# Two graph layers, 16 batches: the partition sums of the first and last batches leave TensorE

## The chip, the cores and the metric

The kernel runs on one core of a Trainium2 chip. Its time is the device time of one launch in microseconds (us). Five engines run their own instruction streams in order: TensorE (PE in the profile), VectorE (DVE), ScalarE (ACT), GpSimd (POOL), and SyncE (SP), which issues the transfers. An engine waits for another only where an instruction needs its result or a buffer that it has still to give back.

## The reference

The input is `x` of 16 batches, 1024 nodes and 256 channels in float32, and one 1024x1024 matrix `adj`. Two layers follow each other in each batch:

```python
# layer 0, per batch
fea  = x.T;  c = mean(fea, axis=channels)
A    = 2*abs(abs(sigmoid(c[None,:]-c[:,None]) - .5) - .5)
Wg   = adj * (A + A.T)/2
q    = relu((fea @ Wg) * para)                # 4 heads of 64
k, v = split(x @ kv_w)
x    = layernorm(x + softmax(q k^T * scale) v)
# layer 1, per batch
h    = relu(x @ w1_loop + adj @ (x @ w1_neigh) + b1)
h    = relu(h @ w2_loop + adj @ (h @ w2_neigh) + b2)
x    = layernorm(x + (x + h)/2)
```

The change concerns the divisors of the softmax (one sum of exponentials for each node and head) and the mean and variance of the first layer's norm (one of each for each node).

## The kernel before

All tensors are cut into tiles of 128 partitions. In layer 0 the norm works in a blocked layout: 128 partitions are four blocks ("quarters") of 32, and a node's channels are spread over the four partitions that have the same place in each block, and over columns. The columns are summed by VectorE. That leaves a `[128, 32]` or `[128, 64]` tile of parts, and one sum over the four quarters is still open, whose result all four need. The divisors of the softmax are spread in the same way, with the two heads of a pair in the two halves of 64 partitions.

There are two ways of closing that sum before the change.

- *By TensorE*, with a constant 128x128 matrix `fold` (L185 to L188) which has a one where two partitions have the same place in their block. `fold_sums` (L283) multiplies a part by it; `denominators` (L862) and `add` (L910) do the same for the divisors and take the reciprocals from PSUM in two halves of 64 partitions (L873, L922). Each such product shows in the profile as two records. The lines are L286, L867 and L916.
- *Without TensorE.* `den_shift` (ScalarE copies each half of 64 partitions to the other half's place in a PSUM tile), `den_halves` (VectorE adds the two), `den_quarters` (four ScalarE copies exchange neighbouring blocks of 32, then VectorE adds and takes the reciprocal), L875 to L897; and `across` (L289), the same pattern for means and variances on GpSimd alone.

One loop over the batches (in `run`, L1456 to L1757) writes out the order of every engine by hand; nothing reorders it. In batch `b`'s turn the kernel works on the attention of batch `b`, the queries, keys and values of batch `b + 1`, and the graph convolutions of batches `b − 1` and `b − 2`, so that TensorE finds work of one while the other engines are at another. The turns are of four kinds, by what neighbours exist:

- batch 0 (`more and not c1`), L1546 and L1654: no convolutions yet; its queries go column by column (`q.step`, products at L633);
- batch 1 (`more and not both`), L1556 and L1712: one convolution;
- batches 2 to 14, L1590 and L1692: the steady turn, which already closes its sums without TensorE;
- batch 15 (`else`), L1650 and L1730: no next batch, so no queries, keys or values.

After the loop come the last convolutions and norms (L1741 to L1757).

Batches 0, 1 and 15 use `fold`: 4, 6 and 4 products. Their places matter. In batch 0 they stand between the query products; the variance's (`norm.variance`, L385) comes just before `kv.sums`, VectorE's four sums for the next keys (L450 to L458), and GpSimd then raises the variance to the power −1/2 (L388) for `norm.scale` (L393). In batch 15 the denominators of the first pair of heads follow the attention outputs (`att.add_pairs(0)`), those of the second pair the first adjacency product of `Joined.run` (L1385), and the mean and variance stand after its products 6 and 7 (the keys 6 and 5 of the dictionary handed to it).

PSUM has two kinds of tiles here: three "big" ones of 1024 columns and two "bank" ones of 512. `scores` (L755) uses both: with `first` given, one score tile in four is split over the two banks (L761 to L763). Scratch for the sums is taken from the banks too.

`Joined.run` computes the two joined convolutions from seven products (numbered 1 to 7) in three PSUM tiles; ScalarE copies each finished product out (L1403 to L1422) so that the tile can be used again, and one of these copies, L1403, puts the loop term of batch `b − 1` into the third tile before product 2 adds to it.

## Time and profile before

| what | value |
|---|---|
| median of 3 runs | 2105.44 us (2105.36 to 2105.63) |
| the profiled execution | 2104.63 us |
| its span | 2102.8 us |
| mean granted TensorE clock | 0.999 of full speed |
| turns of batches 0 and 1 and the start (0 to 320 us) | TensorE busy 317.5, VectorE 286.9, ScalarE 187.2, GpSimd 35.3 us |
| a steady stretch (440 to 560 us) | TensorE 119.9, VectorE 108.1, ScalarE 73.0, GpSimd 28.2 us |
| last turn (1940 to 2062 us) | TensorE 120.4, VectorE 102.3, ScalarE 47.7, GpSimd 17.0 us |

A line of a timeline reads: start in us, busy us, engine, line of the kernel, operation, output <- inputs, partitions x columns, type, count; in brackets the idle time ahead of it and what ended it. Consecutive instructions of one form are drawn together, so "x8" is eight of them. Busy times of neighbours on one engine overlap a little, since an instruction is counted until its last write. The chain of waits is followed back from the last instruction: it gives each engine the share of the span for which it was what the end waited for.

### The profile page before, as it was taken

To read this page: it belongs to the slowest core of one execution; us is meant where nothing else is said; L and a number is where in the kernel's file an instruction comes from. 1 tells how busy PE (TensorE), PEld (TensorE's weight loads), DVE (VectorE), ACT (ScalarE), POOL (GpSimd) and SP (SyncE) were. 2 spreads that over 40 slices of the span, in tenths; PEclk is the share of its full clock that TensorE was granted. 3 is DMA by queue.
4 is the path that set the end of the run, shared out by engine and by line. 5 is a ranking of instruction groups with operands and counts; after the bars stand their busy time and mean duration, and the time that the engine had idled before them with its cause. 6 is when DMAs were issued, how large, how long until landed. Compare 5 with 4: busy or idle time off the path is not lost.

```text
span 2102.8 us, 24938 instructions
## 1 busy us (share of the span) xinstructions
PE 2090.7 (99%) x8282; PEld 988.5 (47%) x8282; DVE 1875.1 (89%) x2238; ACT 1265.9 (60%) x2190; POOL 425.5 (20%) x444
## 2 busy tenths in 40 slices
PE   9999999999999999999999999999999999999998
PEld 5354434445354453544535444354443534445355
DVE  7899998989989899898998989899899998989875
ACT  5844575556756576565755757557575585655523
POOL 2011103122031221213122031220312203122022
PEclk9999999999999999999999999999999999999999
DMA  9495756766648776477864768656586674966455
GB/s 216 122 178 189 145 140 205 138 216 146 173 168 161 242 135 192 151 146 244 142 216 139 135 232 162 230 120 146 206 176 217 143 147 183 185 212 136 137 184 187
DMA packets 688695, 364.99 MB, mean 174 GB/s; under 512 B 550704, under 2 KB 629936, under 8 KB 688560
## 3 DMA queue, kind: packets, MB, share of 16 engines
q1 hardware_dynamic: 688288, 363.07, 66.8%
q8 instruction: 67, 1.10, 0.2%
q14 instruction: 68, 0.56, 0.1%
q10 hardware_dynamic: 272, 0.26, 0.0%
HBM read 305.46 MB, written 57.80 MB: 173 GB/s over the span
## 4 chain that ended last, share of the span: by engine, by line
PE 94%; DVE 4%; issue 1%; DMA 0%; ACT 0%; SPq 0%; DVEq 0%; POOLq 0%; POOL 0%
PE av L815 20%; PE s L769 20%; PE hu_ps L1382 17%; PE g_ps L714 16%; PE v_ps L475 5%; PE k_ps L471 5%; PE hu_ps L1174 4%; PE g_ps L633 3%; PE in_ps L1037 1%; DVE xT L253 1%; DVE den_part L803 1%; DVE acc L790 1%; PE h_ps L1085 1%; PE u_ps L1114 1%; PE h_ps L1174 1%
## 5 line engine op out<-in xcount | busy, mean ns | idle before, releaser
L790 DVE TENSOR_TENSOR acc<-acc,pr 128x1024 f32<-128x1024 f32 x384 | 481.3, 1253 | 34.0 <-ACT pr L776 0.5
L769 PE MATMUL s<-qT,kT 64*128 64x512 f32 x2048 | 452.2, 594 | 1.6 <-DVE in L1054 0.7
L815 PE MATMUL av<-pr,v 128*64 128x512 f32 x2048 | 447.0, 594 | 0.0
L776 ACT ACTIVATE pr<-s 128x1024 f32<-128x1024 f32 x392 | 392.7, 1119 | 60.0 <-PE s L769 60.0
L769 PEld LDWEIGHTS s<-qT,kT 64*128 64x128 f32 x2048 | 194.2, 187 | 247.1 <-issue 186.6
L815 PEld LDWEIGHTS av<-pr,v 128*64 128x64 f32 x2048 | 144.1, 137 | 297.3 <-issue 265.7
L1382 PE MATMUL hu_ps<-adj,R 128*128 128x512 f32 x480 | 213.6, 592 | 0.0
L625 DVE SCALAR_TENSOR_TENSOR wg<-wg,adj 128x1024 f32<-128x1024 f32 x128 | 167.9, 1350 | 3.6 <-ACT wg L620 3.6
L774 ACT ACTIVATE pr<-s 128x512 f32<-128x512 f32 x240 | 142.6, 705 | 0.0
L619 ACT ACTIVATE wg<-c_row,c_sums 128x1024 f32<-128x1024 f32 x120 | 139.4, 1162 | 3.0 <-DVE accB L797 1.0
L1382 PEld LDWEIGHTS hu_ps<-adj,R 128*128 128x128 f32 x480 | 90.0, 190 | 107.1 <-issue 105.7
L620 ACT ACTIVATE wg<-wg 128x1024 f32<-128x1024 f32 x128 | 135.4, 1057 | 4.1
L388 POOL TENSOR_TENSOR rstd<-rstd,neg_half 128x32 f32<-128x32 f32 x16 | 88.3, 5520 | 147.4 <-DVE rstd L385 146.3
L1235 POOL TENSOR_TENSOR rstd<-rstd,neg_half 128x8 f32<-128x8 f32 x12 | 19.7, 1640 | 440.4 <-DVE rstd L1234 440.4
L714 PE MATMUL g_ps<-wg,x 128*128 128x512 f32 x224 | 107.7, 593 | 0.0
L1373 POOL TENSOR_TENSOR R<-h 128x512 f32<-128x512 f32 x14 | 19.6, 1397 | 435.3 <-PE av L815 408.7
L1382 PE MATMUL hu_ps<-adj,t 128*128 128x512 f32 x240 | 107.1, 598 | 0.0
L714 PE MATMUL g_ps<-T,xB 128*128 128x512 f32 x208 | 106.2, 592 | 0.0
L714 PE MATMUL g_ps<-wg,xB 128*128 128x512 f32 x208 | 106.2, 592 | 0.0
L788 DVE TENSOR_TENSOR acc<-pr,pr 128x1024 f32<-128x1024 f32 x64 | 78.0, 1218 | 14.8 <-ACT pr L776 14.8
L797 DVE STREAM_TRANSPOSE accB<-acc 128x1024 f32<-128x1024 f32 x64 | 79.7, 1245 | 3.5 <-PE av L815 0.5
L880 ACT COPY den<-den_part 64x64 f32<-64x64 f32 x26 | 5.5, 210 | 122.7 <-DVE den_part L803 122.2
(316 smaller groups left out, 3339.3 us busy)
## 6 DMA issues: line engine op xcount, KB each, us to landing
adj<-adjT SPq DMA_DIRECT2D x210, 512.0 KB
adj<-in_adj_dram SPq DMA_DIRECT2D x128, 512.0 KB
para<-in_L_gnn_para_dram SPq DMA_DIRECT2D x32, 512.0 KB
xB_a<-in_x_dram SPq DMA_DIRECT2D x128, 128.0 KB
x1d<-xB_a SPq DMA_DIRECT2D x128, 128.0 KB
x<-x1d SPq DMA_DIRECT2D x16, 1024.0 KB
xB<-in_x_dram SPq DMA_DIRECT2D x120, 128.0 KB
x<-in_x_dram SPq DMA_DIRECT2D x15, 1024.0 KB
```

The costliest lines, as they stand in the source:

```text
L471: nc.tensor.matmul(dst, self.a[0][n], self.w[n], start=not again, stop=True, skip_group_check=again)
L475: nc.tensor.matmul(dst[:, ts(t, P)], self.w[n][:, ts(t, P)], self.a[1][n], start=not again and t == 0, stop=True, skip_group_check=again o ...
L619: nc.scalar.activation(wg, self.c_row, AF.Abs, bias=self.c_col[:, t:t + 1], scale=-1.0)
L620: nc.scalar.activation(wg, wg, AF.Tanh, scale=-0.5 / C)
L625: nc.vector.scalar_tensor_tensor(wg, wg, 1.0, self.adj.pop(t), op0=ALU.add, op1=ALU.mult)
L714: nc.tensor.matmul(self.p[n], x_n[:, k, :], w_n, start=(k == 0), stop=(k == TJ - 1))
L769: nc.tensor.matmul(halves[s], self.kT[rows, pair, ts(mt, P)], self.qT[rows, pair, ts(j, FB)], start=True, stop=True)
L774: nc.scalar.activation(pr[:, ts(s, FB)], halves[s], AF.Exp)
L776: nc.scalar.activation(pr, ps, AF.Exp)
L790: nc.vector.tensor_add(self.acc, self.acc, prs[mt])
L815: nc.tensor.matmul(pav[s * HD:(s + 1) * HD, :], self.v[:, mt, pair * P + s * HD:pair * P + (s + 1) * HD], prs[mt][:, ts(s, FB)], start=(mt ...
L1382: nc.tensor.matmul(dst, self.x[n][:, k, :], of_rows(rows, k), start=(start and k == 0), stop=(k == TJ - 1), skip_group_check=again)
```

## The change

The constant matrix `fold` and the three functions that multiply by it are removed. Batches 0, 1 and 15 close their sums without TensorE:

- the divisors by `den_shift`, `den_halves`, `den_copies` and `den_inverse` (the last two were `den_quarters`), now for any two or four of the four units;
- the means by a new class `Quarters`, the same pattern for one 32-column part: two ScalarE copies, a VectorE add, four ScalarE copies, a VectorE add;
- the variances by `across` on GpSimd in batches 0 and 1 (the scaling by 1/C and the added epsilon on GpSimd as well), and by `Quarters` in batch 15.

The pieces of a chain are written at different places of the order, with other work between them. Two names change with it (`squares_aside` and its scratch tile). Batches 2 to 14 issue the same instructions as before.

```diff
-    def fold_sums(part, name, psum_tile=bank_psum):
-        pm = psum_tile(f"{name}_ps")
-        nc.tensor.matmul(pm[:, 0:NB], fold..., part[:, 0, :], start=True, stop=True)
-        return pm[:, 0:NB]
+    class Quarters:
+        def shift(self):
+            self.bank = bank_psum(f"{self.name}_ps")
+            h = P // 2
+            for s in range(2):
+                nc.scalar.copy(self.bank[s * h:(s + 1) * h, 0:NB], self.part[(1 - s) * h:(2 - s) * h, 0, :])
+        def halves(self):
+            nc.vector.tensor_add(self.part[:, 1, :], self.part[:, 0, :], self.bank[:, 0:NB])
+        def copies(self):
+            for a in range(Q):
+                b = a ^ 1
+                nc.scalar.copy(self.bank[a * S:(a + 1) * S, NB:2 * NB], self.part[b * S:(b + 1) * S, 1, :])
+        def total(self):
+            nc.vector.tensor_add(self.part[:, 0, :], self.part[:, 1, :], self.bank[:, NB:2 * NB])
+            return self.part[:, 0, :]
...
     # batch 1, first half of the turn
                 att.scores(1)
-                kv.sums()
-                att.add(0)
+                att.den_shift(0, 2)
+                kv.first_sums()
+                att.den_halves(0, 2)
+                kv.second_sums()
                 att.outputs(1)
...
                 c1.inner()
+                att.den_copies(0, 2)
...
-                c1.first(quarters, lambda: (att.add(1), adj_sums(quarters, 1), adj_sums(quarters, 2), weigh_first()))
+                att.den_inverse(0, 2)
+                att.add(0, 1)
+                adj_sums(quarters, 1)
+                adj_sums(quarters, 2)
+                c1.first(quarters)
+                weigh_first()
...
-                att.add(2)
                 att.outputs(3)
+                att.den_shift(2, 2)
...
     # batch 15, first half
-                att.both_units(1, third=lambda: att.add_pairs(0))
+                def first_outputs():
+                    att.den_shift(2, 2)
+                    att.add_output(0)
+                    att.den_halves(2, 2)
+                    att.den_copies(2, 2)
+                    att.sum_output(0)
+                    att.den_inverse(2, 2)
+                att.den_shift(0, 2)
+                att.den_halves(0, 2)
+                att.den_quarters(0, 2)
+                att.both_units(1, third=first_outputs)
...
     # batch 0, second half
-                for t in range(3, NT):
+                for t in range(3, 6):
                     q.likeness(t)
+                att.den_shift()
+                q.likeness(6)
                 tiles[2] = adj_blocked(2)
                 q.times_adj(3)
                 q.step(0)
+                att.den_halves()
+                att.den_copies()
+                q.likeness(7)
                 q.times_adj(4)
+                att.den_inverse()
                 att.add(0, 1)
...
+                means = Quarters(att.sums, "sum1_0")
+                means.shift()
                 q.step(2)
                 q.times_adj(6)
+                means.halves()
+                means.copies()
                 q.step(3)
                 q.times_adj(7)
                 q.step(4)
-                norm.mean()
+                norm.mean(means.total())
...
-                norm.variance()
+                norm.variance(across(norm.part))
                 kv.sums()
...
     # batch 1, second half
+                q.times_adj(2)
+                att.den_halves(2, 2)
+                att.den_copies(2, 2)
...
-                q.step(1, lambda: att.add(3), 5)
+                q.step(1)
+                att.den_inverse(2, 2)
+                att.add(2, 3)
+                means = Quarters(att.sums, "sum1_1")
+                means.shift()
+                q.times_adj(3)
+                means.halves()
+                means.copies()
...
-                kT, v = kv.run(lambda: (first(), norm.variance()), q.scale, second)
+                norm.variance(across(norm.part))
+                kT, v = kv.run(first, q.scale, second)
...
     # batch 15, second half
-                both.run({1: (lambda: att.add_pairs(1), att.watch), 6: (norm.mean, norm.squares, norm.sum_squares),
-                          5: (lambda: norm.variance(bank_psum),), 4: (norm.scale,), 0: (norm.spread,)}, last=nc.vector)
+                means, variances = (Quarters(part, f"sum{k}_{b}") for k, part in enumerate((att.sums, norm.part)))
+                both.run({1: (lambda: att.add_output(1), lambda: att.sum_output(1), means.shift, att.watch, means.halves,
+                              means.copies),
+                          6: (lambda: norm.mean(means.total()), norm.squares, norm.sum_squares,
+                              variances.shift, variances.halves, variances.copies),
+                          5: (lambda: norm.variance(variances.total(), nc.vector),), 4: (norm.scale,), 0: (norm.spread,)}, last=nc.vector)
```

More of the change, by code (lines that the diff above doesn't have):

```diff
@@ L183 @@
     nc.gpsimd.memset(ones_sb, 1.0)
-    fold = const.tile([P, Q, S], F32, name="fold")
-    nc.vector.tensor_reduce(fold[:, 0, :], ident.rearrange("p (i k) -> p k i", k=S), AX.X, ALU.add)
-    for a in range(1, Q):
-        nc.vector.tensor_copy(fold[:, a, :], fold[:, 0, :])
     c_sums = const.tile([P, S + NT], F32, name="c_sums")
@@ L281, in first_row @@
         return c_row
-    def fold_sums(part, name, psum_tile=bank_psum):
-        pm = psum_tile(f"{name}_ps")
-        nc.tensor.matmul(pm[:, 0:NB], fold.rearrange("p a k -> p (a k)"), part[:, 0, :], start=True, stop=True)
-        return pm[:, 0:NB]
     def across(part):
@@ L297, in across, with __init__ @@
         return part[:, 0, :]
+    class Quarters:
+        def __init__(self, part, name):
+            self.part, self.name = part, name
+        def shift(self):
[12 more added lines that the diff above has]
+            return self.part[:, 0, :]
     def join(part):
@@ L358, with __init__, mean @@
     class BlockedNorm:
-        def __init__(self, xB, sums, name):
-            self.xB, self.sums, self.name = xB, sums, name
-        def mean(self, joined=None):
+        def __init__(self, xB, name):
+            self.xB, self.name = xB, name
+            self.part = small.tile([P, NC, NB], F32, tag="part", name=f"sq_part_{self.name}", bufs=2)
+        def mean(self, joined):
             mean = small.tile([P, NB], F32, tag="mean", name=f"mean1_{self.name}", bufs=2)
-            nc.vector.tensor_scalar_mul(mean, fold_sums(self.sums, f"sum1_{self.name}") if joined is None else joined,
-                                        1.0 / C)
+            nc.vector.tensor_scalar_mul(mean, joined, 1.0 / C)
             for cc in range(NC):
@@ L377, in sum_squares @@
         def sum_squares(self):
-            self.part = small.tile([P, NC, NB], F32, tag="part", name=f"sq_part_{self.name}", bufs=2)
             for cc in range(NC):
@@ L381, in sum_squares, with variance @@
             join(self.part)
-        def variance(self, psum_tile=half_psum, joined=None):
+        def variance(self, joined, eng=nc.gpsimd):
             self.rstd = small.tile([P, NB], F32, tag="rstd1", name=f"rstd1_{self.name}", bufs=2)
-            (nc.vector if joined is None else nc.gpsimd).tensor_scalar(
-                self.rstd, fold_sums(self.part, f"sum2_{self.name}", psum_tile) if joined is None else joined,
-                1.0 / C, EPS, op0=ALU.mult, op1=ALU.add)
+            eng.tensor_scalar(self.rstd, joined, 1.0 / C, EPS, op0=ALU.mult, op1=ALU.add)
             nc.gpsimd.tensor_tensor(self.rstd, self.rstd, neg_half, ALU.pow)
@@ L854, in both_units @@
             settle()
-        def add_pairs(self, *pairs):
-            self.denominators(*pairs)
-            for pair in pairs:
-                self.add_output(pair)
-                self.sum_output(pair)
-        def denominators(self, *pairs):
-            b, half, n = self.b, FB // S, NJ * len(pairs)
-            u0 = NJ * pairs[0]
-            pd = bank_psum(f"den_ps_{b}_{u0}")
-            den = pd[:, 0:n * NB]
-            nc.tensor.matmul(den, fold.rearrange("p a k -> p (a k)"),
-                             self.part[:, u0:u0 + n, :].rearrange("p u k -> p (u k)"), start=True, stop=True)
-            den = den.rearrange("p (u s h) -> p u s h", u=n, s=2)
-            rden = self.rden[:, u0 * half:(u0 + n) * half].rearrange("p (u h) -> p u h", u=n)
-            for s in range(2):
-                rows = slice(s * HD, (s + 1) * HD)
-                nc.vector.reciprocal(rden[rows], den[rows, :, s, :])
@@ L875, in den_shift, with den_parts @@
-        def den_shift(self):
-            self.den = bank_psum(f"den_{self.b}")
-            part = self.part.rearrange("p u (s h) -> p u s h", s=2)
+        def den_parts(self, u0, n):
+            h = FB // S
+            return (self.part[:, u0:u0 + n, :].rearrange("p u (s h) -> p u s h", s=2),
+                    self.den[:, 0:n * h], self.den[:, n * h:2 * n * h], self.rden[:, u0 * h:(u0 + n) * h])
+        def den_shift(self, u0=0, n=len(UNITS)):
+            self.den = bank_psum(f"den_{self.b}_{u0}")
+            part, first, _, _ = self.den_parts(u0, n)
@@ L878, in den_shift, with den_halves @@
             for s in range(2):
                 mine, other = slice(s * HD, (s + 1) * HD), slice((1 - s) * HD, (2 - s) * HD)
-                nc.scalar.copy(self.den[mine, 0:NC * NB].rearrange("p (u h) -> p u h", u=len(UNITS)),
-                               part[other, :, s, :])
-        def den_halves(self):
-            part = self.part.rearrange("p u (s h) -> p u s h", s=2)
+                nc.scalar.copy(first[mine].rearrange("p (u h) -> p u h", u=n), part[other, :, s, :])
+        def den_halves(self, u0=0, n=len(UNITS)):
+            part, first, _, rden = self.den_parts(u0, n)
@@ L885, in den_halves @@
             for s in range(2):
                 mine = slice(s * HD, (s + 1) * HD)
-                nc.vector.tensor_add(self.rden[mine].rearrange("p (u h) -> p u h", u=len(UNITS)),
-                                     self.den[mine, 0:NC * NB].rearrange("p (u h) -> p u h", u=len(UNITS)),
-                                     part[mine, :, s, :])
-        def den_quarters(self):
-            other = self.den[:, ts(1, NC * NB)]
+                nc.vector.tensor_add(rden[mine].rearrange("p (u h) -> p u h", u=n),
+                                     first[mine].rearrange("p (u h) -> p u h", u=n), part[mine, :, s, :])
@@ L893, in den_quarters, with den_copies, den_inverse @@
+        def den_copies(self, u0=0, n=len(UNITS)):
+            _, _, second, rden = self.den_parts(u0, n)
             for a in range(Q):
                 b = a ^ 1
-                nc.scalar.copy(other[a * S:(a + 1) * S], self.rden[b * S:(b + 1) * S])
-            nc.vector.tensor_add(self.rden, self.rden, other)
-            nc.vector.reciprocal(self.rden, self.rden)
+                nc.scalar.copy(second[a * S:(a + 1) * S], rden[b * S:(b + 1) * S])
+        def den_inverse(self, u0=0, n=len(UNITS)):
+            _, _, second, rden = self.den_parts(u0, n)
+            nc.vector.tensor_add(rden, rden, second)
+            nc.vector.reciprocal(rden, rden)
@@ L899, in add_output, with den_quarters @@
+        def den_quarters(self, u0=0, n=len(UNITS)):
+            self.den_copies(u0, n)
+            self.den_inverse(u0, n)
         def add_output(self, pair):
@@ L910, in add @@
         def add(self, *units):
-            b, half = self.b, FB // S
-            u0, n = units[0], len(units)
-            pd = bank_psum(f"den_ps_{b}_{u0}")
-            den = pd[:, 0:2 * half * n]
-            nc.tensor.matmul(den, fold.rearrange("p a k -> p (a k)"),
-                             self.part[:, u0:u0 + n, :].rearrange("p u k -> p (u k)"), start=True, stop=True)
-            den = den.rearrange("p (u s h) -> p u s h", u=n, s=2)
-            rden = self.rden[:, u0 * half:(u0 + n) * half].rearrange("p (u h) -> p u h", u=n)
-            for s in range(2):
-                rows = slice(s * HD, (s + 1) * HD)
-                nc.vector.reciprocal(rden[rows], den[rows, :, s, :])
-            for k, u in enumerate(units):
+            half = FB // S
+            for u in units:
                 pair, j = UNITS[u]
                 o = by_node(self.o.pop(u))
-                nc.vector.tensor_mul(o, o, rden[:, k, :].unsqueeze(2).to_broadcast([P, half, S]))
+                nc.vector.tensor_mul(o, o, self.rden[:, ts(u, half)].unsqueeze(2).to_broadcast([P, half, S]))
                 dst = by_node(self.xB[pair][:, ts(j, FB)])
@@ L1222, in sums_aside, with variancesaside @@
                 nc.scalar.activation(self.x[:, t, :], self.x[:, t, :], AF.Identity, accum_out=self.mv[:, t, 0:1])
-        def squares_aside(self):
+        def variancesaside(self):
             self.centred = True
             nc.vector.tensor_scalar_mul(self.mv[:, :, 0], self.mv[:, :, 0], -1.0 / C)
-            scratch = work.tile([P, FB], F32, tag="o", name=f"squares_{self.b}")
+            scratch = work.tile([P, FB], F32, tag="o", name=f"variances{self.b}")
             for t in range(NT):
@@ L1596, in sums @@
                     if c3:
-                        c3.squares_aside()
+                        c3.variancesaside()
                     c2.load_x()
@@ L1651, in run @@
                 c1.fast_inner(att.both_units(0, c1.load_inner, summed=c1.inner_sums))
-                att.both_units(1, third=lambda: att.add_pairs(0))
-            norm = BlockedNorm(xB, att.sums, str(b))
+                def first_outputs():
[9 more added lines that the diff above has]
+                att.both_units(1, third=first_outputs)
+            norm = BlockedNorm(xB, str(b))
             if more and not c1:
@@ L1712, in run @@
             elif more:
-                q.pair(2)
-                q.step(0)
-                q.step(1, lambda: att.add(3), 5)
-                q.pair(3)
-                q.step(2, norm.mean)
+                q.times_adj(2)
+                att.den_halves(2, 2)
+                att.den_copies(2, 2)
+                q.times_adj(TJ + 2)
+                q.right(2)
+                q.step(0)
+                q.step(1)
[6 more added lines that the diff above has]
+                means.copies()
+                q.times_adj(TJ + 3)
+                means.total()
+                q.right(3)
+                norm.mean(att.sums[:, 0, :])
+                q.step(2)
                 q.load_para()
```

## The prediction

> **What bounds the kernel now.** I read the page's busy shares first, then the chain that ended last, then the timelines of the engines around the 14 products with the constant matrix.

> ```profile
> PE 2090.7 (99%) x8282; PEld 988.5 (47%) x8282; DVE 1875.1 (89%) x2238; ACT 1265.9 (60%) x2190; POOL 425.5 (20%) x444
> PE 94%; DVE 4%; issue 1%; DMA 0%; ACT 0%; SPq 0%; DVEq 0%; POOLq 0%; POOL 0%
> ```

> TensorE is busy 99% and carries 94% of the chain. So a product taken away is worth the time by which the next one starts sooner, and a new wait of TensorE costs its length. VectorE, at 89%, is the only other engine near its limit; ScalarE (60%) and GpSimd (20%) have time, but each runs its queue in order. The granted clock is 0.999 and plays no part.

> A product and its neighbours on TensorE's timeline of batch 15:

> ```profile
> 1974.03 14.00 PE L769 MATMUL s<-qT,kT 64*128 64x512 f32 x64
> ...
> 2001.85 0.43 PE L867 MATMUL den_ps<-den_part,fold 128*128 128x64 f32 x2
> 2002.12 3.65 PE L1382 MATMUL hu_ps<-adj,t 128*128 128x512 f32 x8
> ...
> 2005.78 3.65 PE L1382 MATMUL hu_ps<-adj,t 128*128 128x512 f32 x8
> ...
> 2020.37 3.68 PE L1382 MATMUL hu_ps<-adj,h 128*128 128x512 f32 x8
> ```

> The columns are start, busy time, engine, line, operation and count. The denominators' product (L867) delays the next work by 0.27, from 2001.85 to 2002.12; those of batch 0 (L916) by 0.17 and a gap of 0.05 to 0.1 before them.

> **What the change removes.** Against the pitch of the neighbouring matmuls (eight 128x512 records in 3.44), the four products of batch 0 cost TensorE 0.96, the six of batch 1 1.58 and the four of batch 15 1.38, of which 0.21 is a wait. Were all of it kept, the time would fall by 3.9. Batches 2 to 14 keep their order and waits: 0.

> **Batch 0.** The two denominator products become one ScalarE/VectorE chain, and the mean another. VectorE loses four half-height reciprocals and gets two adds, a full add, a reciprocal and two small adds for the mean: about equal. ScalarE's twelve copies (0.21 to 0.24 each by batch 2's rows below) stand among query work; ScalarE is busy 187 of the first 320 us, so I cost them at nothing. If that cover is gone they cost up to their 2.5.

> The variance is another matter. These are VectorE's rows, then GpSimd's of batch 2, where the same sum is already made, once slowly and once fast:

> ```profile
> 128.24 0.19 DVE L300 TENSOR_TENSOR sq_part<-sq_part 128x32 f32<-128x32 f32 x1
> 129.03 0.19 DVE L385 TENSOR_SCALAR rstd<-sum_ps 128x32 f32<-128x32 f32 x1 [0.60 <-PE sum_ps L286]
> 129.14 0.68 DVE L450 TENSOR_TENSOR K<-xT 128x512 f32<-128x512 f32 x1
> 136.97 2.35 DVE L393 TENSOR_TENSOR xB_a<-xB_a,rstd 128x1024 f32<-128x1024 f32 x2
> ```

> ```profile
> 348.96 2.21 POOL L295 COPY sums<-sums 64x32 f32<-64x32 f32 x2 [4.53 <-DVE sums L300]
> 374.88 0.45 POOL L295 COPY sq_part<-sq_part 64x32 f32<-64x32 f32 x2 [21.56 <-DVE sq_part L300]
> 377.38 5.44 POOL L388 TENSOR_TENSOR rstd<-rstd,neg_half 128x32 f32<-128x32 f32 x1
> ```

> VectorE no longer waits 0.60 for the product: its key sums start at about 128.5 instead of 129.14, 0.64 sooner. TensorE's keys and values hang on copies behind VectorE's queries there, so of its 0.96 it keeps 0.64. Against that, the six copies, two adds and the scaling of the variance are now GpSimd's. The fast row takes 2.5 (374.88 to 377.38); the slow one 4.4 (348.96 to 353.3). The power that follows takes 5.44 to 5.84. From 128.5 the result is there at 136.6 at best and 139.1 at worst. Behind it waits VectorE's scaling at L393 (136.97 before), and behind that, in its queue, everything to L590. What decides between the rows is VectorE: under the slow copies it ran operations with both inputs in SBUF (L625), under the fast ones operations reading PSUM. Here the four key sums (L450 to L458, both inputs in SBUF, 2.5 long) come first and PSUM readers after, so I take a value between, 137.9: VectorE is 0.93 late (ends: 0.4 early, 2.2 late). The third score tile needs L588's buffer: TensorE begins the scores at 144.82, four records of 0.2177 a tile, so the third at 146.56, and L588 ends at 145.75; with the hand-over 0.75 is to spare. So TensorE is 0.18 late there (ends: 0.64 early, 1.45 late).

> [...]

> **Batch 1.** Of the 1.58, the first two products' part (0.34 and 0.25) is kept: TensorE arrives at 197.6 with 0.18 − 0.59 = −0.41. From there to 296.03 VectorE runs almost without a pause, and TensorE waits for it at the end:

> ```profile
> 296.73 3.70 PE L769 MATMUL s<-qT,kT 64*128 64x512 f32 x16 [0.68 <-DVE in L1054]
> ```

> So only VectorE's work counts. It loses four half-height reciprocals (0.52 a pair, twice) and the 0.11 of L385: 1.2. It gets two half adds, an add, a reciprocal and the mean's two adds: 1.3. The other products' 0.99 turns into waiting. The variance's parts are joined at 250.92; with GpSimd's 4.4 of the slow row it is summed at 255.3, no later than the 255.44 of before: nothing. Batches 0 and 1 together: −0.41 + 0.1 = −0.3 (ends −1.2 and +0.85).

> **Batch 15**, where the chains stand on the path. Its pieces are in batch 2 already:

> ```profile
> 329.19 0.45 DVE L887 TENSOR_TENSOR rden<-den,den_part 64x64 f32<-64x64 f32 x2
> 329.96 0.92 ACT L895 COPY den<-rden 32x64 f32<-32x64 f32 x4
> ```

> ```profile
> 1975.41 1.24 DVE L1058 STREAM_TRANSPOSE in<-in 128x1024 f32<-128x1024 f32 x1
> 1975.20 1.94 ACT L776 ACTIVATE pr<-s 128x1024 f32<-128x1024 f32 x2 [2.20 <-PE s L769]
> 1989.89 0.83 ACT L1403 COPY hu_ps<-in 128x512 f32<-128x512 f32 x1
> 2005.81 0.58 ACT L1405 COPY snap<-hu_ps 128x512 f32<-128x512 f32 x1 [15.09 <-PE hu_ps L1382]
> 2017.98 0.57 ACT L1417 COPY snap<-hu_ps 128x512 f32<-128x512 f32 x1
> ```

> *Step A, the first pair's denominators.* Their scratch holds one of the two "bank" PSUM tiles until the chain's full add has read it. The third score tile of the next unit is split over both banks; its second half would start at 1974.03 + 10 × 0.2177 = 1976.21. The chain stands behind L1058 on VectorE, which ends at 1976.63: halves 0.4 to 1977.0, four ScalarE copies 0.9 to 1977.9, the add 0.2 and hand-over to 1978.2. TensorE stalls 2.0 (1.6 with the shorter, 32-column, operations; 2.4 with a gap at every hand-over). Queued behind the copies on ScalarE are the exponentials, 1975.20 before, 1977.9 after, 2.7 late; TensorE has about 0.75 in hand on them, which gives 1.95 and comes to the same stall, not another. VectorE's row sums are late by the same 2.7 and 0.7 of it is left over against TensorE's 2.0; that goes into the 1.38 it idles before L848.

> *Step B, the second pair's.* Times now without A's shift. The copies stand on ScalarE in front of the copy that loads a third PSUM tile (L1403, at 1989.89 before, long in time), which the second adjacency product needs. Row sum L803 ends at 2003.79; then the shift, the multiply and add of the first pair (to 2006.1), the halves to 2006.5, four copies to 2007.4, and L1403's 0.6 to 2008.1. That product, at 2005.78 before, now starts at 2008.1: +2.3.

> *Step C, the norm.* The two sum products go (−0.5). The mean is there 0.8 later than before, for its own chain. The variance's six copies (two, a VectorE add, four) stand on ScalarE behind the squares and in front of L1417's copy, which frees the buffer that the product at 2020.37 writes. Squares end near 2018.8, VectorE's join near 2020.3, the six copies near 2021.6, L1417's copy near 2022.2 instead of 2018.55, and the product starts then: +1.83. B's lateness, less the 0.5, comes to the same moment, so B and C cost this once; 0.08 of gaps go: +1.75 (1.4 to 2.3). Scaling is in time after it, and the tail hands the delay on: TensorE's pauses there, of 0.7, are for ScalarE copies that shift with it.

> **Sum.** −0.3 + 2.0 + 1.75 = +3.45 (ends 1.8 and 5.55). The profiled execution's 2104.63 (its span and 1.8 around it) becomes 2108.1. The median of the runs, 2105.44, lies 0.81 above that execution: 2108.9. What this kernel's measurement tells from no change is 0.2%, 4.2 us: slower begins at 2109.65, faster ends at 2101.2.

> **Rivals.** *GpSimd decides (slower).* If batch 0's result comes at the slow end, 139.1, batches 0 and 1 give +0.85 and the sum is +4.6: 2110.0. It ends beyond 0.2% from a result at 138.7 on. For it: the 2.21 row, and four key sums in the way. Against it: they last 2.5, less than the 4.4.
> *ScalarE's chains on time (a little faster).* If the copies of batch 15 reach ScalarE while TensorE still has work ahead, steps A to C cost nothing and all products are won: 2105.44 − 3.9 = 2101.5. It holds if the first chain ends before 1976.2 and L1403's copy before 2005.8. For it: ScalarE idled 15.09 before 2005.81. Against it: the copies wait for VectorE's sums, not for ScalarE, and those ended at 2003.79.
> *One stall of batch 15 hidden.* If the first chain ends before TensorE's third tile, only B and C are left: 2106.9. For it: ScalarE idled 2.20 before 1975.20 and the first pair's sums were there by then. Against it: the halves stand behind L1058.
> *Dearer hand-overs.* If each of the seven hand-overs on the path (three in A, four in B) takes 0.15 more than I took from batch 2, batch 15 costs 4.8 and the sum is +4.5: 2109.9.

> **How the numbers follow.** My forecast 0.56 (2108.9, its own range 2107.7 to 2110), GpSimd 0.14, dearer hand-overs 0.13, one stall hidden 0.12, all on time 0.05. Slower by over 0.2%: most of both dear rivals (0.24) and the upper fifth of my own case (0.12), 0.36. Faster by over 0.2% needs every product won and something more: 0.03. The rest, 0.61, lies within. The range takes in the hidden stall and both dear rivals and leaves out the last: 2106.5 to 2111.0.

> **What would show it.** Right: TensorE pauses of about 2 at the second score unit of batch 15 with a VectorE add of the denominators as releaser, then of about 2.3 before the second adjacency product and little before the fourth. Wrong: no pause at the scores (A falls); the scaling of batch 0 before 136.97 (the GpSimd price falls); a pause in batches 2 to 14.

## The result

| | before | changed |
|---|---|---|
| median of 10 runs | 2105.49 us (2104.77 to 2106.34) | 2111.38 us (2109.38 to 2111.91) |
| profiled execution | 2104.63 us, span 2102.8 | 2109.88 us, span 2107.9 |

The ratio is 1.0025, with a 95% interval of 1.0016 to 1.0035: slower, and more likely than not by more than the 0.2% that was set as the bound, though the interval reaches below that. The forecast was 2108.9, its range 2106.5 to 2111.0: by the ratio (1.0025 × 2105.44 = 2110.7) the time lies inside, by the median 0.4 above. The ten times of the changed kernel lie in two groups, four from 2109.4 to 2109.9 and six from 2111.4 to 2111.9; those of the kernel before do not. The lower group is 4.1 above the kernel before, the upper one 6.0. Two things have to be explained: the 4.1, of which 3.45 was forecast, and the step of 1.8, which was not forecast at all.

The page after, head and busy shares:

```profile
span 2107.9 us, 24933 instructions
PE 2090.0 (99%) x8254; PEld 989.5 (47%) x8254; DVE 1874.5 (89%) x2244; ACT 1276.1 (61%) x2244; POOL 429.7 (20%) x462
```

TensorE has 28 records fewer (14 products), 0.7 us less to do and 5.1 us more span. So it waits more. The waits of TensorE, longest in total (engine, output, line, whom it waited for; then total, times, longest):

```profile
PE hu_ps L1373 <- ACT hu_ps L1394: 2.4, 1, 2.4
PE idle L1457 <- POOL ident masks.py:199: 1.5, 1, 1.5
PE s L779 <- DVE rden L893: 1.2, 1, 1.2
PE s L779 <- DVE kT L598: 0.9, 1, 0.9
PE g_ps L724 <- DVE T L698: 0.7, 1, 0.7
```

The second was there before (a fixed wait at the start). The third and the first are batch 15's, steps A and B of the prediction; the fourth is batch 0's first scores and the last is in batch 1. The two places of batch 15 on TensorE's timeline:

```profile
1974.33 2.84 PE L779 MATMUL s<-qT,kT 64*128 64x512 f32 x10
1978.35 12.28 PE L779 MATMUL s<-qT,kT 64*128 64x512 f32 x54 [1.18 <-DVE rden L893]
1990.56 13.95 PE L825 MATMUL av<-pr,v 128*64 128x512 f32 x64
2004.44 3.70 PE L1373 MATMUL hu_ps<-adj,t 128*128 128x512 f32 x8
2010.58 3.70 PE L1373 MATMUL hu_ps<-adj,t 128*128 128x512 f32 x8 [2.44 <-ACT hu_ps L1394]
2014.12 10.46 PE L1373 MATMUL hu_ps<-adj,R 128*128 128x512 f32 x24
2024.71 3.70 PE L1373 MATMUL hu_ps<-adj,h 128*128 128x512 f32 x8
```

and what stood in ScalarE's queue at these places:

```profile
1977.25 0.81 ACT L889 COPY den<-rden 32x32 f32<-32x32 f32 x4 [3.53 <-DVE rden L882]
1978.01 1.91 ACT L786 ACTIVATE pr<-s 128x1024 f32<-128x1024 f32 x2
2009.10 0.81 ACT L889 COPY den<-rden 32x32 f32<-32x32 f32 x4 [2.24 <-DVE rden L882]
2009.94 0.59 ACT L1394 COPY hu_ps<-in 128x512 f32<-128x512 f32 x1
2024.08 0.57 ACT L1408 COPY snap<-hu_ps 128x512 f32<-128x512 f32 x1
```

The scores stop after exactly ten records, in the middle of the third tile, until VectorE's add of the denominators has released the bank. The copy of the loop term (L1394, which was at 1989.89 before) comes only after the second pair's four copies, and the product needs it.

Because the launches begin with small differences, batch 15 is best measured from its own first score of the second pair to TensorE's last product (the test of the divisors, the last row of TensorE). That stretch is 2095.50 − 1974.03 = 121.47 before and 2099.86 − 1974.33 = 125.53 after: **+4.06**. Matching TensorE's records of the two traces one by one gives the rest: the first products start 0.06 earlier, 0.51 arises between 30 and 60 us, where no instruction had changed, and the part from there through batches 0 and 1 is **−0.43**; a further 0.27 arises in one place near 1386. Together that is the 4.36 by which the last product is late.

### The profile page after: what moved, and what is told of

Its sections match the earlier page's. It is cut to its first block, busy times and chain, and to the rows that moved or that the text cites. A ratio compares the mean times of both kernels' runs of the same rounds, so it can differ in the third digit from the quotient of the medians.

```text
span 2107.9 us, 24933 instructions
## 1 busy us (share of the span) xinstructions
PE 2090.0 (99%) x8254; PEld 989.5 (47%) x8254; DVE 1874.5 (89%) x2244; ACT 1276.1 (61%) x2244; POOL 429.7 (20%) x462
## 5 line engine op out<-in xcount | busy, mean ns | idle before, releaser
L779 PEld LDWEIGHTS s<-qT,kT 64*128 64x128 f32 x2048 | 198.5, 187 | 246.9 <-issue 179.7
L284 POOL COPY sq_part<-sq_part 32x32 f32<-32x32 f32 (+1 forms) x90 | 19.5, 216 | 407.6 <-DVE sq_part L313 404.2
L876 ACT COPY den<-den_part 64x64 f32<-64x64 f32 (+1 forms) x36 | 7.3, 204 | 145.8 <-DVE den_part L813 145.1
```

The source lines that it names most:

```text
L779: nc.tensor.matmul(halves[s], self.kT[rows, pair, ts(mt, P)], self.qT[rows, pair, ts(j, FB)], start=True, stop=True)
```

## The experiments

In the table, "batch 15" is the stretch just defined in each kernel's profiled execution. "Half clock" is the stretch of the profile with a granted TensorE clock of 0.5 that ends before TensorE's last product. (Behind the last product the clock falls to 0.5 too: 2.2 before the end of the span in the kernel before, 3.5 in the changed kernel.)

| kernel | median, us (lowest to highest) | batch 15 | longest pause of TensorE in it | half clock |
|---|---|---|---|---|
| before | 2105.49 (2104.77 to 2106.34) | 121.47 | 0.7 | none |
| changed | 2111.38 (2109.38 to 2111.91) | 125.53 | 2.44 | none |
| again | 2111.01 (2108.97 to 2111.70) | 127.24 | 2.44 | 3.41 |
| b15_kept | 2104.90 (2104.27 to 2106.45) | 121.47 | 0.7 | none |
| b15_only | 2111.06 (2110.24 to 2112.28) | 127.23 | 2.44 | 3.41 |
| reordered | 2104.57 (2103.70 to 2106.11) | 120.12 | 0.7 | none |
| step_a | 2108.28 (2106.86 to 2109.32) | 123.24 | 2.44 | none |
| step_b | 2110.24 (2108.47 to 2111.06) | 125.01 | 2.31 | none |
| pause_13 | 2106.80 (2106.18 to 2108.56) | 122.93 | 1.69 | none |
| pause_26 | 2112.38 (2111.46 to 2112.85) | 128.39 | 4.93 | 6.82 |
| reordered_2 | 2104.54 (2104.02 to 2105.89) | 120.11 | 0.7 | none |
| all_mended | 2104.50 (2103.83 to 2105.64) | 120.34 | 0.7 | none |

### The changed kernel again

No edit.

> The changed kernel once more, to see what its times consist of. Theory (batch 15's chains): TensorE's stalls are part of the order, so every execution has them: 1.2 at the second score unit of batch 15, 2.4 before the second adjacency product, last product 4.1 to 4.4 later than before. The ten times seen lie in two groups, 2109.4 to 2109.9 and 2111.4 to 2111.9; the theory has no name for the step of 1.8 and expects both groups again, median 2109.5 to 2111.5. If this profile falls in the upper group, the step must be a stretch of 1.8 that the first profile lacks. Rival (end of the program): the step lies behind TensorE's last product, which is 7.3 before the end of the span in the kernel before and 8.0 in the changed one: then 9 to 10 here in the upper group, and the products stay in place.

This profile fell in the upper group (2111.70). The pauses are the same to the hundredth, and the time behind the last product is the same 8.0; so the rival, the end of the program, falls. The difference lies in one product: the one after the pause of 2.44 takes 5.40 instead of 3.70.

```profile
2010.71 5.40 PE L1373 MATMUL hu_ps<-adj,t 128*128 128x512 f32 x8 [2.44 <-ACT hu_ps L1394]
2015.95 10.46 PE L1373 MATMUL hu_ps<-adj,R 128*128 128x512 f32 x24
```

The granted clock differs there. In this execution it falls to 0.5 at 2011.16 and is back at 2014.57, 3.41 later. In the changed kernel's first profile it rises at 5.20 and falls at 2104.39, behind the last product: 2099.20 apart, 615 times 3.413; in the kernel before it rises at 4.90 and falls at 2100.68: 2095.78 apart, 614 times 3.413. The windows below have that length. In this execution they are cut at its two changes; in the first profile, where the clock does not change here, they are counted from its rise, and their places are an estimate of mine. The columns are the window, its length, TensorE's busy time (with the records in it), the granted clock, the DMA share and GB/s. First this execution, then the first profile (the lower group):

```profile
2007.75:2011.16 3.41, 0.97 (x3) 1.00 0.40 159
2011.16:2014.57 3.41, 3.41 (x5) 0.50 0.00 0
2014.57:2017.98 3.41, 3.41 (x9) 1.00 0.02 5
```

```profile
2005.41:2008.82 3.41, 2.73 (x7) 1.00 0.98 389
2008.82:2012.23 3.41, 1.65 (x4) 1.00 0.05 19
2012.23:2015.64 3.41, 3.41 (x9) 1.00 0.03 5
```

In this execution the whole pause of 2.44 falls in one such window, which holds 0.97 of work, and the next one runs at 0.50: five records, where the window ahead of the pause has ten, 1.7 lost. In the first profile the boundary at 2008.82 cuts the pause (0.68 before it and 1.76 after it), and the clock stays at 1.00. Same program, same pause, two times.

These are two profiles; for the other executions there is the mean granted clock of each. It reads 0.998 in 5 of the 6 executions of the upper group and in none of the 4 below in the result, and likewise in 5 of 6 (2111.0 and later) and none of 5 here. A mean of 0.998 (below 0.9985 of a span of some 2109) takes more than 6.3 us at half clock, and the stretch behind the last product was 2.2 in the kernel before and 3.5 in the first profile: that those executions had a half clock before it is an estimate from these numbers.

### Batch 15 as before, and batch 15 alone

```diff
 # b15_kept: the changed kernel, with
+                att.both_units(1, third=lambda: att.add_pairs(0))       # products with fold
...
 # b15_only: the kernel before, with first_outputs, Quarters for means and variances as in the change
```

> The changed kernel with batch 15 as it was (its four products with the constant matrix). Theory: batch 15 holds all that TensorE loses (4.06 by the two profiles), batches 0 and 1 give +0.02: last product within 0.4 of before, time 2105 to 2106.3, ratio 0.9998 to 1.0004. Rival 1 (batches 0 and 1, whose first score waits 0.91 for GpSimd's power): +0.8 or more would be left, 2106.3 or later. Rival 2 (what lies behind the last product, 0.7 to 2.5 in the changed kernel, comes with any change of the instruction count): 2106 to 2108 with the products in place.

> The kernel before with only batch 15 changed. Theory: +4.1 on TensorE's last product and 2109.5 to 2110 in time, with the same two stalls of batch 15 (1.2 and 2.4). Rival (batches 0 and 1 carry a part): the last product less than 3.5 late. The end behind the last product tells whether the changed kernel's two groups need batches 0 and 1 too: one group here if so, two if not.

With batch 15 as it was, the stretch is 121.47 again and the median 2104.90; its ratio is 0.9998 (0.9989 to 1.0007), as the theory had it. With batch 15 alone changed, the ratio is 1.0027 (1.0017 to 1.0038), and the stretch is 127.23, of which 1.70 is the half clock that this profile has too (one product of 5.40 for 3.70); without it 125.53, the changed kernel's. Batch 15 holds the whole loss. I expected 2109.5 to 2110.0 for b15_only: all eight runs were later, and four of them have a mean clock of 0.998, so by the same estimate the half clock is not rare there. Whether eight of eight is more than luck against six of ten these runs don't say.

Batches 0 and 1, taken from the record-by-record comparison, give −0.40 to −0.44 in the six profiles whose batches 0 and 1 are those of the change, b15_kept and all_mended left out. In b15_kept they give −0.79, since TensorE waits 0.4 instead of 0.7 for VectorE in batch 1:

```profile
PE s L790 <- DVE kT L609: 0.9, 1, 0.9
PE g_ps L735 <- DVE T L709: 0.4, 1, 0.4
```

The traces show where this begins: at 215.6 VectorE's row sum waits 0.46 for an exponential in the six profiles, and doesn't in b15_kept and all_mended. Why it does stayed open.

The 0.27 near 1386 divides the profiles in the same way: it is in those six, and in none of the other six. There GpSimd's copies of a mean and VectorE's weighting of the adjacency matrix start almost together, VectorE first in the kernel before, GpSimd first in the changed one:

```profile
1381.66 2.38 DVE L625 SCALAR_TENSOR_TENSOR wg<-wg,adj 128x1024 f32<-128x1024 f32 x2
1381.87 2.23 POOL L295 COPY sums<-sums 64x32 f32<-64x32 f32 x2 [4.52 <-DVE sums L300]
```

```profile
1381.90 1.45 POOL L284 COPY sums<-sums 64x32 f32<-64x32 f32 x2 [4.52 <-DVE sums L313]
1382.06 2.37 DVE L635 SCALAR_TENSOR_TENSOR wg<-wg,adj 128x1024 f32<-128x1024 f32 x2 [0.29 <-issue]
```

VectorE's rows behind it are 0.4 late, and TensorE's product there 0.27. That the one leads to the other is read from the rows, not tested, and what turns the order round stayed open.

### The same work in another order

```diff
-                att.den_shift(0, 2)
-                att.den_halves(0, 2)
-                att.den_quarters(0, 2)
-                att.both_units(1, third=first_outputs)
+                att.both_units(1, lambda: att.den_shift(0, 2), lambda: (att.den_halves(0, 2), att.den_copies(0, 2)),
+                               third=first_outputs, fourth=lambda: att.den_inverse(0, 2))      # A
...
                 def first_outputs():
+                    both.prepare()      # B: the copy of the loop term into the third PSUM tile
                     att.den_shift(2, 2)
...
-                          6: (lambda: norm.mean(means.total()), norm.squares, norm.sum_squares,
-                              variances.shift, variances.halves, variances.copies),
+                          6: (lambda: norm.mean(means.total()), norm.squares, norm.sum_squares),
+                          7: (variances.shift, variances.halves, variances.copies),             # C
```

`first` and `second` run between VectorE's row sums of the last unit, after every exponential is issued on ScalarE, and `fourth` (a new place) after two more of the sums.

> The changed kernel with the same instructions in batch 15, three of its chains issued elsewhere: the first pair's denominators behind the exponentials of the last two score units, the copy of the loop term ahead of the second pair's copies, and the variance's copies behind the copy of product 7. Theory (the place on ScalarE's queue and of the bank is the cause, not the work): both stalls of 1.2 and 2.4 vanish, and the product after product 5 is not later; what is late next is GpSimd's power, which ends near 2028 against 2026.3 before and then holds VectorE's scaling: last product from 0.9 earlier to 0.8 later than before, time 2104.6 to 2106.5. Rival (the work itself is too much for ScalarE and VectorE there): new stalls of the same size, time above 2108.5.

The stretch is 120.12 and, in a second profile, 120.11: not only are the 4.06 gone, it is 1.35 shorter than before, which is the 1.38 that the four products cost. Both new pauses of TensorE in batch 15 vanish (the 0.7 in the table is in the kernel before too):

```profile
1974.59 14.00 PE L779 MATMUL s<-qT,kT 64*128 64x512 f32 x64
2002.41 7.13 PE L1376 MATMUL hu_ps<-adj,t 128*128 128x512 f32 x16
2009.38 10.46 PE L1376 MATMUL hu_ps<-adj,R 128*128 128x512 f32 x24
2019.68 3.60 PE L1376 MATMUL hu_ps<-adj,h 128*128 128x512 f32 x8
```

What I named as late next is late, but by so little that TensorE doesn't see it; VectorE's scaling waits 1.30 for GpSimd's power:

```profile
2027.58 2.36 DVE L403 TENSOR_TENSOR xB_a<-xB_a,rstd 128x1024 f32<-128x1024 f32 x2 [1.30 <-POOL rstd L398]
```

So the work was never too much for ScalarE and VectorE; its place was wrong. The medians are 0.9 under the kernel before in both sessions, but the ratios, 0.9996 (0.9987 to 1.0005) and 0.9994 (0.9985 to 1.0003), don't exclude no change.

### One step at a time

step_a is edit A of the diff above alone, step_b edit B alone.

> The changed kernel, only the first pair's denominators moved behind the exponentials of the last two score units. Theory: the pause of 1.2 at the scores and the 0.5 that ScalarE's lateness adds go (2.3 in all), the pause of 2.4 before the second adjacency product stays; the step of 1.7, which in the profile of the second look is a stretch of 3.4 with half the clock at the end of that pause, stays too. Two groups, near 2107.3 and 2109.0, median 2107 to 2109. Rival (the two stalls hide behind one another): the second pause grows by what the first loses, time as the changed kernel's.

> The changed kernel, only the copy of the loop term moved ahead of the second pair's copies. Theory (B and C come to one moment): the pause of 2.4 before the second adjacency product goes, and 2.4 to 3.0 appear before the product that waits for the copy of product 7, which stands behind the variance's copies; last product within 0.3 of the changed kernel's, the clock's step now after that pause, time 2109.5 to 2111.7. Rival (a stall that goes is gained): -2.2 and no half clock, 2107.3, one group.

step_a gains 125.53 − 123.24 = 2.29 of the stretch, the 2.3 expected; the pause of 2.44 stays, and the runs lie in two groups again (five from 2106.9 to 2107.4, all with a mean clock of 0.999, six from 2108.3 to 2109.3, all with 0.998). Step B was not hiding step A.

step_b loses its pause before the second adjacency product, and has this instead:

```profile
2025.18 3.70 PE L1374 MATMUL hu_ps<-adj,h 128*128 128x512 f32 x8 [2.31 <-ACT snap L1415]
```

It gains 0.52 of the stretch where 2.44 of pause went: the product that waits for the copy behind the variance's chain was due at almost the same moment. That is what step C said, and it is why the prediction counted B and C once. I had put the stretch within 0.3 of the changed kernel's; it is 0.5 shorter. Its times lie in two groups too (2108.5 to 2109.3 and 2110.2 to 2111.1), but not by the clock alone: its profile, 2110.24, has no half clock before the last product. There TensorE waits 1.2 for the first input transfer, and batch 15 begins 1.29 later than in the kernel before. So the time of a single execution doesn't tell what made it long.

### A pause by itself

To separate the clock from the change, the kernel before, with its products, gets nothing but small copies in front of the copy of the loop term:

```diff
                 both.fetch(1, 4, "11")
+                for _ in range(13):       # pause_26: 26
+                    nc.scalar.copy(att.part[:, 0, :], att.part[:, 3, :])
                 both.run({1: (lambda: att.add_pairs(1), att.watch), ...
```

> The kernel before, with 13 more small ScalarE copies (0.22 each) in front of the copy of the loop term in batch 15, behind the last row sum: nothing of the change, only a pause of TensorE before the second adjacency product, 1.3 to 1.7 long. They overwrite a part that has been used. Theory of the clock (a pause of over some 2 within 3.4 halves the clock for 3.4, a shorter one doesn't): +1.3 to +1.7, one group, 2106.8 to 2107.3, clock 1 throughout. Rival (any pause of TensorE costs more than its length): more than 2.2 over the kernel before in some executions.

> The same with 26 copies: a pause of 4.0 to 4.5. Theory of the clock: half the clock after the pause in every execution, at a cost of 0.4 to 1.7 by where its stretch of 3.4 begins: time 2110.2 to 2111.9, none at the pause's length alone. Rival (the slow matmuls of the changed kernel come from its new PSUM copies beside them, which this kernel has not): clock 1, 2109.4 to 2110.0, one group.

A pause of 1.69 costs 1.46 of the stretch. Ten of the eleven runs lie from 2106.2 to 2107.3, one at 2108.56, of which there is no profile. That one is 3.1 above the kernel before, as the rival said of some executions; its mean clock reads 0.999 like the others', and whether a half clock or something else lengthened it stays open. A pause of 4.93 (I had reckoned 4.0 to 4.5) costs 6.92, and every run is later than 2111.4; the median, 2112.38, lies above the 2111.9 that I had set as the upper end. Its clock:

```profile
2005.23:2008.64 3.41, 0.80 (x4) 1.00 0.35 135
2008.64:2012.05 3.41, 1.09 (x2) 0.50 0.01 2
2012.05:2015.46 3.41, 3.41 (x6) 0.50 0.00 0
2015.46:2018.87 3.41, 3.41 (x10) 1.00 0.00 0
```

The window at 1.00 holds 0.80 of work, and the half clock behind it lasts 6.82: through a window that holds 1.09 of work and through the next one, full of work. The rival, that the slow matmuls come from the change's own PSUM copies beside them, falls: this kernel has none of them. And 2.44 before a product at full clock in one execution and at half in another, with the same program, leaves one difference seen: where the pause lay, all of it within 2007.75 to 2011.16 in the one at half clock, on both sides of 2008.82 by my count in the other.

### Batch 0's variance without GpSimd

```diff
-                norm.variance(across(norm.part))
+                variances = Quarters(norm.part, "sum2_0")
+                variances.shift()
+                variances.halves()
+                variances.copies()
+                norm.variance(variances.total(), nc.vector)
                 kv.sums()
```

on top of the reordered kernel, which ran beside it once more.

> The reordered kernel again, to stand beside the next one on the same chip: 2104.0 to 2105.2, TensorE's wait of 0.9 for VectorE at the first scores of batch 0 in place.

> The reordered kernel, and batch 0's variance summed by ScalarE and VectorE in the way of the means, instead of by GpSimd (the power stays there). Theory (GpSimd's sum, 4.0 long beside the key sums, is what makes the power late): the power ends near 136.6 instead of 138.5, the wait of 0.9 at the first scores goes, and as VectorE's work of batch 1 starts behind TensorE's scores there, 0.5 to 0.9 of it is kept to the end: 2103.4 to 2104.2, and faster than the kernel before by 1.2 to 2. Rival (batch 1 is bound by VectorE, which gives back what batch 0 wins): the wait goes, the waits on VectorE at 242 and 296 grow by the same, time within 0.2 of the reordered kernel's.

Both theories fell. The wait of 0.9 at the first scores goes, but the chain now stands in VectorE's queue in front of the key sums, with its two round trips to ScalarE:

```profile
129.34 0.19 DVE L301 TENSOR_TENSOR sq_part<-sq_part,sum_ps 128x32 f32<-128x32 f32 x1 [0.46 <-ACT sum_ps L298]
130.41 0.19 DVE L309 TENSOR_TENSOR sq_part<-sq_part,sum_ps 128x32 f32<-128x32 f32 x1 [0.88 <-ACT sum_ps L306]
```

The key sums start at 130.73 (128.78 in the changed kernel), the queries behind them are late, and TensorE, which had no wait there, has two:

```profile
PE k_ps L481 <- DVE qT L654: 0.8, 1, 0.8
PE k_ps L481 <- ACT ksnap L537: 0.7, 1, 0.7
```

Batches 0 and 1 give −0.09 here, where they gave −0.41 in the reordered kernel. The medians are the same (2104.50 and 2104.54), as the rival had said, but not by its road: TensorE's wait in batch 1 is 0.4 here and didn't grow, and the 0.27 near 1386 is absent, which makes up for most of the loss. The same mistake as batch 15's, made by me: the chain was put in the queue in one piece where its waits had work behind them.

## Why the prediction was right or wrong

- **Direction and place: right.** The loss is batch 15's (b15_kept, b15_only), by ScalarE's queue and the bank, not by the amount of work (reordered).
- **Step A: right in mechanism, 0.3 short.** The stall at the third tile's second half, predicted for 1978.2 from 1976.21, is 1978.35 from 1976.51: 1.84, against 2.0. But the second road, the late exponentials, which I said "comes to the same stall, not another", adds 0.46 over the next tiles: 2.30 in all. The term was mis-sized by taking the larger of the two where a part of the second comes on top. (step_a takes both away together, 2.29; that the 0.46 comes by the second road is read from the times of the records, not tested apart.)
- **Step B and C together: right.** Predicted +1.75; the changed kernel has 4.06 − 2.30 = 1.76. That the two come to one moment is shown by step_b, where undoing B alone gives 0.5.
- **Batch 0: right in mechanism.** GpSimd's sum, put between 2.5 and 4.4, took 4.0 (129.02 to 132.99, its rows below). The ends that the prediction gave for the power's result, 136.6 and 139.1, are 0.2 and 0.4 later than 128.5 and its own rows add up to (136.4 and 138.7); no row is given for the rest. Its ends for batches 0 and 1, −1.2 and +0.85, leave out the 0.1 that its sum has. This profile runs 0.45 behind the one before when it comes to batch 0's change (0.51 from 30 to 60 us, less 0.06 at the start), so 0.45 is taken off what follows. VectorE's key sums started at 128.78 instead of 129.14: 0.81 sooner (0.64 predicted). The scaling started at 138.50 instead of 136.97: 1.08 late (0.93). The third score tile started at 147.34 instead of 146.56: 0.33 late (0.18).

```profile
129.02 1.24 POOL L284 COPY sq_part<-sq_part 64x32 f32<-64x32 f32 x2 [79.25 <-DVE sq_part L313]
130.98 1.29 POOL L284 COPY sq_part<-sq_part 32x32 f32<-32x32 f32 x4
132.99 5.48 POOL L398 TENSOR_TENSOR rstd<-rstd,neg_half 128x32 f32<-128x32 f32 x1
138.50 2.36 DVE L403 TENSOR_TENSOR xB_a<-xB_a,rstd 128x1024 f32<-128x1024 f32 x2 [1.82 <-POOL rstd L398]
```

  The first pair of half copies, 0.45 and 2.21 in the two rows of batch 2, took 1.24 beside the key sums, and the whole sum's 4.0 lies between the 2.5 and the 4.4 of those rows, nearer the slow one.
- **Batches 0 and 1: right.** −0.3 predicted, −0.43 measured. TensorE arrives at the attention outputs behind batch 1's second scores 0.20 early (201.81 against 201.56, less 0.45), where 0.41 was predicted, and ends the two batches 0.13 better than predicted.
- **Batches 2 to 14: put at 0, found +0.27.** Their order is as it was, but at one place, near 1386, VectorE and GpSimd start in the other order and TensorE is later by that much.
- **The sum: 3.45 predicted, 3.9 found** (−0.43 + 0.27 + 4.06), and 4.1 between the lower group and the kernel before. Step A's 0.3 and the 0.27 near 1386, less the 0.13 of batches 0 and 1, are the difference.
- **Wrong: what a pause costs.** The prediction said that "a new wait of TensorE costs its length" and that the granted clock "plays no part". For a pause of 2.44 it held in the first profile of the changed kernel (clock 1.00, 3.70 for the next product) and not in the second, which pays 1.7 on top (clock 0.50 for 3.41, 5.40 for that product); by the mean clock, an estimate, so do most of the upper groups, 6 of 10 and 6 of 11 runs. This sets the median, 2111.38 instead of about 2109.6, and takes the time, more likely than not, to slower by more than 0.2%, the case to which 0.36 was given. That the time by the ratio still lies in the range is luck: its upper end was drawn for two dear rivals that did not come. None of the rivals had the clock; "dearer hand-overs" gave a like time for another reason, and the hand-overs were not dearer (step A's chain took 1.84 for the 2.0 predicted).

What the windows show: those at 1.00 that held 0.97 (again and b15_only) and 0.80 us of TensorE's work (pause_26) had one at 0.50 behind them; those that held 1.65 (changed), 1.73 (pause_13) and 1.77 (step_a), their places an estimate as above, had one at 1.00. Between 0.97 and 1.65 these windows show nothing. A pause of 2.44, shorter than the 3.41 of a window, came to both; the forecast pause of 2.3 lies near it.

## What to carry to other kernels

Taking small products off a busy engine paid here only where the chain that replaces them has its round trips with no urgent work behind them in the queues: the same instructions in batch 15 cost 4.06 in one order and won 1.35 in another. When a stall is removed, look for what was due at the same moment (step_b won 0.5 for 2.44), and when one is forecast on TensorE, look at the granted clock behind it: 1.69 of pause cost 1.46 in one profile (pause_13, clock 1.00), 4.93 cost 6.92 (pause_26, 0.50 for 6.82), and 2.44 cost 1.7 more in one execution of the changed kernel than in another (0.50 for 3.41 against 1.00).
